# Layer norm 1 of an attention block: the loads of x on another queue, and the order of all engines by hand up to the first values

## The chip, the core and the metric

The kernel runs on one core of a Trainium2 chip. A core has five engines with instruction streams of their own: TensorE (PE in the profile, its weight loads apart as PEld), VectorE (DVE), ScalarE (ACT), GpSimd (POOL) and SyncE (SP), which here only issues DMAs. ACT and GpSimd can issue DMAs as well. The metric is the device time of one execution in microseconds (us), the median of several runs; less is better.

## What is computed

The reference is a network of two layers on x of shape (4, 16, 16, 1024) in float32, seen as 1024 tokens of 1024 channels. What matters for the change is the seam between them:

```python
x = x + conv_attention(group_norm(x), ...)      # layer 0: its last step is a sum of two products per token tile
t = to_tokens(x)                                # 1024 tokens x 1024 channels
t = t + attention(layer_norm(t), W_attn, b_attn, W_proj, b_proj)   # layer 1
t = t + experts(layer_norm(t), ...)             # 8 experts, gates under a threshold are dropped
```

In `attention`, q, k and v are products of the normalised tokens with the three parts of `W_attn`; v is computed first. The result is `y @ W_proj.T + b_proj`, added to t.

## The kernel before, in words

The tokens are handled in eight tiles of 128; tile `t = 2 * b + nt` is half `nt` of image `b`. Layer 0 ends with position terms that are moved by many small DMAs within the chip's memory (`move`, L472, on SP's queue, from `two_T` to `s0`), with a v product of seven half-size products (L513 to L556, the Strassen-Winograd scheme, which reads `xn` and `w_kv`), and then with the loop L575.

Ahead of that loop, x itself is loaded again, one tile per DMA (L564, SP's queue), into memory that `xn` held; so a load can start only when the last v product has read `xn`. The loop goes over the tiles in the order of `tiles` (all tiles with nt = 1, then those with nt = 0). For the tile at place i it does:

- `content` (L437) for the next tile: four products whose results DVE adds to `s0` (L445). For i = 0 it does the first tile's too.
- the spread products `py` (L586): eight matrix products in two banks of PSUM, which DVE adds to x (L593).
- `layer_norm` (L184): statistics on DVE, a square root on ACT between two small DVE steps (`inverse_root`, L131), and the normalising on ACT. The rows have to be turned, so that channels lie on partitions. For the first six tiles the rows are written to DRAM (L207), read back as four quarters (`quarters_of`, L174; both on SP's queue), and turned on DVE in blocks of 32 (`turn`, L179) two tiles later. For the last two, PE transposes them (L202) and ACT copies them out (L203).
- GpSimd adds the bias `b_proj` of the output projection to x (L603) and writes the result to DRAM (`x_rows`, L604), from where it comes back late in layer 1 (L877).

In this loop SP and DVE keep the order in which the code stands (`manual_schedule`); PE, ACT and GpSimd are ordered by a planner. After it, `project_v` (L650) computes v for two halves of the weights, r = 0 and 1. Each is again done with seven products per pair of token tiles: products 1 and 2 need only weights and tokens, 3 to 7 need sums. The sums of weights (`sums_of_A`, L151) are four DVE operations of 128x1024 for each r and are issued after the last layer norm. The sums of tokens (`sums_of_B`, L630) are four DVE operations of 128x2048, and write `T`, which lies where x lay. Each bank goes through `product` (L638), which takes turns between the tags `mm` and `tr`, three banks each. The weights `w_v` are loaded by SP (L121 through L648); the second of them takes the memory of `ln_rows`.

The steps 28 to 33 of layer 1's loop (L867) load x back and run the output projection (`project_out`, L821), which adds its product to x (L827).

```python
            for t in in_time:
                c11, c12, c21, c22 = homes(t)
                nc.scalar.copy(c22, one(t, 1, a11, b11))
                nc.vector.tensor_add(c11, one(t, 2, a12, b21), c22)
            if r == 0:
                sums_of_B()
```

Of the kernel before, what the change touches and what calls it, by code (L numbers as in the profile page):

```python
# [32 lines left out]
F32 = mybir.dt.float32  # L33
I32 = mybir.dt.int32
AF = mybir.ActivationFunctionType
ALU = mybir.AluOpType
# [3 lines left out]
P = 128  # L40
C = 1024
NC = C // P
B = 4
M = 256
# [18 lines left out]
Q = 4  # L63
# [6 lines left out]
def kernel(  # L70
# [54 lines left out]
    def mm(name):  # L125
        return ps.tile([P, HALF], F32, tag="mm", name=name)

    def tr(name):
        return ps.tile([P, HALF], F32, tag="tr", name=name)
# [21 lines left out]
    def sums_of_A(a11, a12, a21, a22, s1, s2, s4):  # L151
        nc.vector.tensor_add(s1, a21, a22)
        nc.vector.tensor_sub(s2, s1, a11)
        nc.vector.tensor_sub(s4, a12, s2)
        nc.vector.tensor_sub(a21, a21, a11)
# [28 lines left out]
    def layer_norm(ln, t, dst, quarters, turns):  # L184


        stats = small.tile([P, 2, 6], F32, tag="ln_stats", name=f"ln1_stats{t}")
        for j in range(2):
            nc.vector.bn_stats(stats[:, j, :], xs[t][:, ts(j, HALF)])
        mv = small.tile([P, 2], F32, tag="ln_mv", name=f"ln1_mv{t}")  # L190
        nc.vector.bn_aggr(mv, stats)
        rstd = small.tile([P, 1], F32, tag="ln_rstd", name=f"ln1_rstd{t}")
        inverse_root(rstd, mv[:, 1:2], EPS)
        if quarters is None:
            less = small.tile([P, 1], F32, tag="ln_less", name=f"ln1_less{t}")
            done = nc.vector.scalar_tensor_tensor(less, mv[:, 0:1], -1.0, rstd, ALU.mult, ALU.mult)
            for j in range(2):
                nc.scalar.activation(ln[:, ts(j, HALF)], xs[t][:, ts(j, HALF)], AF.Identity, bias=less, scale=rstd)
            for j in range(2):
                pt = tr(f"ln1_pt{t}_{j}")  # L200
                for c in range(4):
                    nc.tensor.transpose(pt[:, ts(c, P)], ln[:, (4 * j + c) * P : (4 * j + c + 1) * P], ident)  # L202
                nc.scalar.copy(dst[:, 4 * j : 4 * j + 4, ts(t, P)], pt.rearrange("p (c n) -> p c n", c=4))  # L203
            return done
        done = normalised(ln, xs[t], mv[:, 0:1], rstd)
        rows = turns.tile([P, Q, C // Q], F32, tag="rows", name=f"ln1_rows{t}")
        nc.sync.dma_start(rows.rearrange("n f c -> n (f c)"), ln)  # L207
        quarters_of(rows, quarters)
        return done


    with ExitStack() as layer0:
# [347 lines left out]
        xs = [x_at[:, t, :] for t in range(NT)]  # L560
        tiles = [(b, nt) for nt in (1, 0) for b in range(B)]
        for b, nt in tiles:
            t = 2 * b + nt
            nc.sync.dma_start(xs[t], x[ts(t, P), :])  # L564
# [9 lines left out]
        with tc.manual_schedule(engines={mybir.EngineType.SP, mybir.EngineType.DVE}):  # L574
            for i, (b, nt) in enumerate(tiles):  # L575
                if i == 0:
                    content(b, nt)
                if i + 1 < NT:
                    content(*tiles[i + 1])
                t = 2 * b + nt  # L580
                for hp in range(2):
                    py = mm(f"py{t}_{hp}")
                    for hl in range(2):
                        bh = b * HEADS0 + 2 * hp + hl
                        for mh in range(2):
                            nc.tensor.matmul(  # L586
                                py[:, ts(hl, M)],
                                s0[:, mh, ts(nt, S2), :, bh].rearrange("p i j -> p (i j)"),
                                v_T[:, mh, ts(b, M)],
                                start=(mh == 0),  # L590
                                stop=(mh == 1),
                            )
                    nc.vector.tensor_add(xs[t][:, ts(hp, HALF)], xs[t][:, ts(hp, HALF)], py)  # L593

                quarters = None
                if i < NT - 2:
                    quarters = tpool.tile([P, Q, C // Q], F32, tag="xg", name=f"ln1_quarters{t}")
                to_turn.append((t, quarters))
                ln_done = layer_norm(ln_rows[:, i % 3, :], t, ln1, quarters, turns)
                if i >= 2:  # L600
                    of, quarters = to_turn[i - 2]
                    turn(ln1[:, :, ts(of, P)], quarters)
                nc.gpsimd.tensor_add(xs[t], xs[t], bp)  # L603
                nc.gpsimd.dma_start(x_rows[ts(t, P), :], xs[t])  # L604
    x_home.close()


    with ExitStack() as attention:
        l1, l1w = pool(attention, "l1"), pool(attention, "l1w", 2)
        turns = attention.enter_context(tc.tile_pool(name="turns", bufs=3, space=bass.MemoryType.DRAM))  # L610
        mask = l1.tile([P, 3, P], F32, tag="mask", name="mask")
        nc.gpsimd.memset(mask[:, 1, :], 0.0)
        make_causal_mask(nc, mask[:, 0, :], NEG)
        make_causal_mask(nc, mask[:, 2, :], NEG)
        bqk = l1.tile([P, 2 * NPAIR], F32, tag="bqk", name="bqk")
        nc.gpsimd.dma_start(bqk, b_qk)
        step_qk = l1.tile([P, NPAIR], F32, tag="step_qk", name="step_qk")
        nc.gpsimd.tensor_sub(step_qk, bqk[:, NPAIR:], bqk[:, :NPAIR])

        bv = l1.tile([P, NPAIR], F32, tag="bv", name="bv")  # L620
        nc.gpsimd.dma_start(bv, b_v.rearrange("(n p) -> p n", p=P))
        v1 = [l1.tile([P, NT, M], F32, tag=f"v1_{g}", name=f"v1_{g}") for g in range(4)]


        sums = ExitStack()
        s_pool = pool(sums, "s_pool", 2, side="right")
        T = [s_pool.tile([P, NC // 2, HALF], F32, tag=f"T{i}", name=f"T{i}", bufs=1) for i in range(3)]
        b11, b12, b21, b22 = (ln1[:, 4 * j : 4 * j + 4, ts(l, HALF)] for j in range(2) for l in range(2))

        def sums_of_B():  # L630
            nc.vector.tensor_sub(T[0], b12, b11)
            nc.vector.tensor_sub(T[1], b22, T[0])
            nc.vector.tensor_sub(b12, b12, b22)
            nc.vector.tensor_sub(T[2], b21, T[1])
# [3 lines left out]
        def product(name, stationary, moving, n):  # L638
            nonlocal n_products
            n_products += 1  # L640
            bank = (mm if n_products % 2 else tr)(name)[:, :n]
            for c in range(NC // 2):
                nc.tensor.matmul(bank, stationary(c), moving(c), start=(c == 0), stop=(c == NC // 2 - 1))  # L643
            return bank


        s_v = big_tile(0, "s_v", (2, 3, NC // 2, M))
        w_v = [w_tile(f"w_v{r}", W_attnT[:, 2 * C + r * HALF : 2 * C + (r + 1) * HALF]) for r in range(2)]  # L648

        def project_v(r):  # L650
            a = [w_v[r][:, 4 * j : 4 * j + 4, ts(i, M)] for i in range(2) for j in range(2)]
            a11, a12, s3, a22 = a
            s1, s2, s4 = (s_v[:, r, i, :, :] for i in range(3))
            with tc.issue_after(ln_done.ins):
                sums_of_A(*a, s1, s2, s4)

            def one(t, n, a, b):
                return product(f"pv{r}_{t}_{n}", lambda c: b[:, c, ts(t, P)], lambda c: a[:, c, :], M)

            def homes(t):  # L660
                return [v1[2 * r + i][:, 4 * l + t, :] for i in range(2) for l in range(2)]

            in_time = (1, 3, 0, 2)
            for t in in_time:
                c11, c12, c21, c22 = homes(t)
                nc.scalar.copy(c22, one(t, 1, a11, b11))  # L666
                nc.vector.tensor_add(c11, one(t, 2, a12, b21), c22)
            if r == 0:
                sums_of_B()

            for t in in_time:
                nc.scalar.copy(homes(t)[1], one(t, 3, s4, b22))
            for t in range(4):
                c11, c12, c21, c22 = homes(t)
                nc.vector.tensor_add(c22, one(t, 6, s2, T[1]), c22)
                nc.vector.tensor_add(c21, one(t, 7, s3, b12), c22)
                nc.vector.tensor_add(c12, c12, c22)
                p5 = one(t, 5, s1, T[0])
                nc.vector.tensor_add(c12, p5, c12)
                nc.vector.tensor_add(c22, p5, c21)  # L680
                nc.vector.tensor_add(c21, one(t, 4, a22, T[2]), c21)
# [134 lines left out]
        project_v(0)  # L816
        project_v(1)
# [48 lines left out]
        with tc.manual_schedule():  # L866
            for i in range(written, len(steps) + lag):  # L867
                if i == written:
                    w_p.append(w_tile("w_p0", W_projT[:, :HALF]))
                if i == 28:  # L870
                    w_p.append(w_tile("w_p1", W_projT[:, HALF:]))
                    sums.close()
                    x_pool = pool(x_home, "xb", side="right")
                    xs = [x_pool.tile([P, C], F32, tag=f"x{t}", name=f"xb{t}") for t in range(NT)]
                if 28 <= i < 32:
                    for t in range(2 * (i - 28), 2 * (i - 28) + 2):
                        nc.gpsimd.dma_start(xs[t], x_rows[ts(t, P), :])  # L877
                s_T = turned_s.pop(i - lag)
# [19 lines left out]
                if i == 22:  # L898
                    sums_qk(7)

# [693 lines left out]
```

## Time and profile before

| | before |
|---|---|
| median of 3 runs | 1251.93 us (1250.96 to 1254.14) |
| the profiled execution | 1253.85 us |
| its span in the profile | 1252.0 us |
| PE busy | 1225.3 us (98%) |
| DVE busy | 744.2 us (59%) |
| ACT busy | 220.2 us (18%) |
| GpSimd (POOL) busy | 383.3 us (31%) |
| mean granted TensorE clock | 0.993 |
| stretch of the loop over tiles | about 206 to 277 us |
| first product on weight sums | 297.82 us |

How to read the lines of the profile. A timeline row has the start, the duration, the engine (SPq and ACTq are DMA issues on SP's and ACT's queues), the line of the kernel, the operation, what is written <- what is read, and the count of merged instructions; in brackets stands the idle time just before it and what ended it. PE rows count one float32 product of the code as two records. A row of the windows table has the stretch, its length, the busy time and count of PE, PEld, DVE, ACT and POOL, the granted TensorE clock (1.00 is full), the mean share in which the 16 DMA engines were busy, and GB/s.

### The profile page before, as it was taken

The page shows a single profiled execution, that of the slowest core. Times are in us where ns is not written, and L with a number is a line of the kernel's source. Part 1 is how long each engine was busy: PE and PEld are TensorE (multiplying, and loading weights), DVE is VectorE, ACT ScalarE, POOL GpSimd, SP SyncE. Part 2 cuts the span into 40 slices and gives each one's busy share as a digit, 9 for nine tenths or more (in the row PEclk, how much of TensorE's full clock was granted, in tenths as well). Part 3 has the DMA queues.
Part 4 walks back from the last instruction along what each step waited for, and adds up shares of the span by engine and source line. Part 5 has one row for each costly group of instructions (what it writes and reads, how often), then busy time and mean ns, then how long its engine had stood idle before and what let it go on. Part 6 is the DMA issues. An engine that isn't in the chain of part 4 may idle for free.

```text
span 1252.0 us, 13310 instructions
## 1 busy us (share of the span) xinstructions
PE 1225.3 (98%) x4796; PEld 633.7 (51%) x4796; DVE 744.2 (59%) x1337; ACT 220.2 (18%) x514; POOL 383.3 (31%) x455
## 2 busy tenths in 40 slices
PE   9999999699999999999999999999999999999998
PEld 5445885477885444444444444444344434434443
DVE  5796535487332566666644866864746646565642
ACT  3310111121000222232212422110110111111110
POOL 0141340241000222223231104445543635363520
PEclk9999999889999999999999999999999999999999
DMA  9002023862202344453283558374756485546442
GB/s 348 20 1 84 1 56 74 308 202 101 68 1 68 98 134 133 136 169 113 96 262 119 190 201 285 73 224 94 235 126 190 101 236 151 150 124 197 101 84 53
DMA packets 93977, 169.25 MB, mean 135 GB/s; under 512 B 11952, under 2 KB 48832, under 8 KB 93904
## 3 DMA queue, kind: packets, MB, share of 16 engines
q1 hardware_dynamic: 76544, 115.83, 28.1%
q0 software_dynamic: 15136, 47.78, 16.1%
q10 hardware_dynamic: 2224, 4.72, 1.1%
q8 instruction: 40, 0.66, 0.2%
q14 instruction: 33, 0.27, 0.1%
HBM read 115.59 MB, written 48.50 MB: 131 GB/s over the span
## 4 chain that ended last, share of the span: by engine, by line
PE 74%; DVE 2%; ACT 1%; issue 0%; DVEq 0%; ACTq 0%
PE p L1361 31%; PE pqk L643 16%; PE pv L643 7%; PE po L825 7%; PE left L1403 3%; PE sc L738 2%; PE pa L807 2%; PE rest L1417 2%; PE last_pe L1519 1%; PE dense_pe L945 1%; PE parts L1083 0%; ACT L134 0%; DVE row_T L179 0%; DVE xb L827 0%; DVE T L1304 0%
## 5 line engine op out<-in xcount | busy, mean ns | idle before, releaser
L930 POOL DMA_INDIRECT w_e_xg<-rows,gather x146 | 157.0, 1076 | 57.5 <-issue 39.9
L1361 PE MATMUL p<-w_e,A 128*128 128x512 f32 x368 | 163.2, 593 | 1.3 <-DVE slot L1196 1.3
L780 POOL TENSOR_TENSOR s_q<-s_q,total 128x128 f32<-128x128 f32 (+1 forms) x128 | 66.0, 546 | 301.0 <-DVE total L777 301.0
L825 PE MATMUL po<-w_p,y_T 128*128 128x512 f32 x256 | 118.5, 605 | 0.0
L1361 PEld LDWEIGHTS p<-w_e,A 128*128 128x128 f32 x368 | 69.6, 190 | 89.9 <-issue 89.4
L1361 PE MATMUL p<-T,S 128*128 128x512 f32 x256 | 112.7, 593 | 0.0
L953 POOL DMA_INDIRECT out_dram<-y,add x32 | 56.5, 1766 | 177.4 <-ACT y L1367 114.1
L1367 ACT ACTIVATE y<-y,slot 128x512 f32<-128x512 f32 x64 | 46.1, 722 | 334.6 <-DVE y L1375 175.9
L766 ACT ACTIVATE s_q<-s,top 128x256 f32<-128x256 f32 (+1 forms) x128 | 56.6, 443 | 186.1 <-issue 146.7
L643 PE MATMUL pqk<-ln,w_qk 128*128 128x512 f32 x192 | 85.6, 595 | 0.0
L1361 PEld LDWEIGHTS p<-T,S 128*128 128x128 f32 x256 | 48.6, 190 | 60.8 <-issue 60.5
L825 PEld LDWEIGHTS po<-w_p,y_T 128*128 128x128 f32 x256 | 45.9, 190 | 47.9 <-issue 46.9
L179 DVE STREAM_TRANSPOSE A<-w_e_xg 128x1024 f32<-128x1024 f32 x32 | 39.6, 1239 | 47.8 <-DMA w_e_xg<-rows,gather 47.8
L643 PE MATMUL pqk<-T,S_qk 128*128 128x512 f32 x128 | 58.5, 599 | 0.0
L643 PEld LDWEIGHTS pqk<-ln,w_qk 128*128 128x128 f32 x192 | 36.0, 190 | 43.3 <-issue 42.3
L1361 PE MATMUL p<-w_e,S 128*128 128x512 f32 x128 | 57.5, 592 | 0.0
L1361 PE MATMUL p<-T,A 128*128 128x512 f32 x128 | 57.5, 592 | 0.0
L643 PE MATMUL pv<-w_v,ln 128*128 128x256 f32 x192 | 45.6, 391 | 0.5 <-ACT v L666 0.5
L304 PE MATMUL pq<-w_q,xn 128*128 128x512 f32 x96 | 44.5, 599 | 0.3 <-ACT xn L284 0.3
L603 POOL TENSOR_TENSOR x_at<-x_at,ln_rows 128x1024 f32<-128x1024 f32 x8 | 19.4, 2427 | 78.5 <-ACT ln_rows L162 73.4
L1403 PE MATMUL left<-w_e,one 128*32 128x512 f32 x312 | 41.8, 593 | 0.0
L643 PEld LDWEIGHTS pv<-w_v,ln 128*128 128x128 f32 x192 | 37.3, 196 | 6.4 <-ACT v L666 1.2
(318 smaller groups left out, 1869.2 us busy)
## 6 DMA issues: line engine op xcount, KB each, us to landing
w_e<-in_expert_w_dram SPq DMA_DIRECT2D x14, 2048.0 KB, 12.5
s_rows<-s_q SPq DMA_DIRECT2D x32, 384.0 KB, 2.4
s_rows<-s_rows SPq DMA_DIRECT2D x128, 96.0 KB, 2.3
w_qk<-in_W_attnT_dram SPq DMA_DIRECT2D x8, 1024.0 KB, 5.9
xn<-in_xT_dram SPq DMA_DIRECT2D x8, 512.0 KB, 7.6
w_q<-in_Wq_dram SPq DMA_DIRECT2D x16, 256.0 KB, 7.3
x_at<-in_x_dram SPq DMA_DIRECT2D x8, 512.0 KB, 6.5
w_v<-in_W_attnT_dram SPq DMA_DIRECT2D x2, 2048.0 KB, 13.4
```

The costliest lines, as they stand in the source:

```text
L179: nc.vector.transpose(row_T[:, :, :slots].rearrange("p c (g j) -> p g c j", j=32), row[:, : slots // 32, :].rearrange("p g (c i) -> p g c ...
L304: nc.tensor.matmul(pq, xn[:, c, ts(t, P)], w_q[kc][:, c, :], start=(c == 0), stop=(c == NC - 1))
L643: nc.tensor.matmul(bank, stationary(c), moving(c), start=(c == 0), stop=(c == NC // 2 - 1))
L738: nc.tensor.matmul(psc[:, h, qt * P : qt * P + (qt + 1) * P], qk[pair][part, 0, b * M + qt * P : b * M + (qt + 1) * P], qk[pair][part, 1, ...
L766: nc.scalar.activation(blocks(h, qt), s[:, h, cols].rearrange("p (b f i) -> p b f i", f=Q, i=32), AF.Exp, bias=top[:, qt, h : h + 1], accu ...
L780: nc.gpsimd.tensor_mul(blocks(h, qt), blocks(h, qt), total[:, qt, h : h + 1].unsqueeze(2).unsqueeze(3).to_broadcast([P, 1 + qt, Q, 32]),)
L825: nc.tensor.matmul(po, y_T[:, c, ts(t, P)], w_p[j][:, c, :], start=(c == 0), stop=(c == NC - 1))
L930: nc.gpsimd.indirect_dma_start(out=row[:, g, :], out_offset=None, in_=table[: (TOK - P) * Q, :] if e in SHORT else table, in_offset=bass.I ...
L953: nc.gpsimd.indirect_dma_start(out=out[: TOK - P, :] if e in SHORT else out, out_offset=bass.IndirectOffsetOnAxis(ap=add[:slots, e, k : k ...
L1361: nc.tensor.matmul(bank, a[:, c, :], b[:, c, :], start=(c == 0), stop=(c == NC // 2 - 1))
L1367: nc.scalar.mul(y[i][:, ts(j, HALF)], y[i][:, ts(j, HALF)], slot[:, e, 1, 2 * pair + i : 2 * pair + i + 1])
L1403: nc.tensor.matmul(bank[ts(i, 32), :], stationary, w[of][j][:, c, :], start=(c == 0), stop=(c == NC - 1))
```

## The change

- The eight loads of x are issued by ACT and no longer by SP.
- The order by hand covers all engines, and reaches from the loop over tiles to the end of r = 0 of the values and the start of GpSimd's work for r = 1 (`in_order`).
- `layer_norm` is cut into parts: the norm itself, `turn_by_rows`, `turn_on_pe` and `turned_on_pe`. The loop runs over seven tiles; the eighth is done by steps in between the first products of the values: products 1 and 2 for tiles 1 and 3, then the transposes of the seventh tile, products for tile 0, the transposes of the eighth, products for tile 2.
- The sums of weights are done by GpSimd (`sums_v`), those for r = 0 right after the last spread products, the others later. The mask and the small bias loads of GpSimd stand after the first of them.
- The sums of tokens are done in two halves (`sums_of_B(1)`, `sums_of_B(0)`), eight operations in place of four.
- The quarters of the first four tiles use memory of layer 0 that is free (`spare`), the next two a pool of their own (`late`).
- For the last two tiles in the order, x is written to `x_rows` by SP right after the spread products, without the bias. GpSimd adds the bias after x has come back, at steps 32 and 33; the bias is loaded once more at step 28.
- The first `w_v` load stands ahead of the loop in the code; `w_v1` comes after the transposes.

The diff, cut to its core:

```diff
-    def sums_of_A(a11, a12, a21, a22, s1, s2, s4):
-        nc.vector.tensor_add(s1, a21, a22)
...
+    def sums_of_A(a11, a12, a21, a22, s1, s2, s4, engine=nc.vector):
+        engine.tensor_add(s1, a21, a22)
...
+    def turn_by_rows(ln, t, quarters, turns):
         rows = turns.tile([P, Q, C // Q], F32, tag="rows", name=f"ln1_rows{t}")
         nc.sync.dma_start(rows.rearrange("n f c -> n (f c)"), ln)
         quarters_of(rows, quarters)
...
+    def turn_on_pe(ln, banks):
+
+        for j, pt in enumerate(banks):
+            for c in range(4):
+                nc.tensor.transpose(pt[:, ts(c, P)], ln[:, (4 * j + c) * P : (4 * j + c + 1) * P], ident)
+
+    def turned_on_pe(dst, t, banks):
+        for j, pt in enumerate(banks):
+            nc.scalar.copy(dst[:, 4 * j : 4 * j + 4, ts(t, P)], pt.rearrange("p (c n) -> p c n", c=4))
...
+        late = pool(x_home, "late", 2, side="right")
...
-            nc.sync.dma_start(xs[t], x[ts(t, P), :])
+            nc.scalar.dma_start(xs[t], x[ts(t, P), :])
...
-        with tc.manual_schedule(engines={mybir.EngineType.SP, mybir.EngineType.DVE}):
...
+        w_v = [w_tile("w_v0", W_attnT[:, 2 * C : 2 * C + HALF])]
+        in_order.enter_context(tc.manual_schedule())
+        for i in range(NT - 1):
+            t = spread(i)
+            quarters = None
+            if i < NT - 2:
+                if i < NT - 4:
+                    quarters = spare[i % 2]
+                else:
+                    quarters = late.tile([P, Q, C // Q], F32, tag="xg", name=f"ln1_quarters{t}")
+            to_turn.append((t, quarters))
+            layer_norm(ln_rows[:, i % 3, :], t, i >= NT - 2)
+            if i >= 2:
+                turn_quarters(i - 2)
+            if i < NT - 2:
+                turn_by_rows(ln_rows[:, i % 3, :], t, quarters, turns)
                 nc.gpsimd.tensor_add(xs[t], xs[t], bp)
                 nc.gpsimd.dma_start(x_rows[ts(t, P), :], xs[t])
+            else:
+                nc.sync.dma_start(x_rows[ts(t, P), :], xs[t])
+        t = spread(NT - 1)
+        nc.sync.dma_start(x_rows[ts(t, P), :], xs[t])
+        s_v = big_tile(0, "s_v", (2, 3, NC // 2, M))
...
+        def first(r, t, *tags):
+            nc.scalar.copy(homes(r, t)[3], one(r, t, 1, *tags[:1]))
+            return r, t, one(r, t, 2, *tags[1:])
+
+        def second(r, t, bank):
+            c11, c12, c21, c22 = homes(r, t)
+            nc.vector.tensor_add(c11, bank, c22)
...
+        sums_v(0, nc.gpsimd)
+        seconds = [first(0, 1, tr, tr), first(0, 3, mm, tr)]
+        layer_norm(ln_rows[:, (NT - 1) % 3, :], t, True)
+        two = ps.tile([P, 2, HALF], F32, tag="sc", name="ln_two", bufs=1)
+        banks = two[:, 0, :], two[:, 1, :]
+        turn_on_pe(ln_rows[:, (NT - 2) % 3, :], banks)
+        turned_on_pe(ln1, to_turn[NT - 2][0], banks)
+        turn_quarters(NT - 3)
+        for done in seconds:
+            second(*done)
+        second(*first(0, 0, mm, mm))
+        banks = tr("ln_pt0"), mm("ln_pt1")
+        turn_on_pe(ln_rows[:, (NT - 1) % 3, :], banks)
+        turned_on_pe(ln1, t, banks)
+        second(*first(0, 2, tr, tr))
+        x_home.close()
...
+        w_v.append(w_tile("w_v1", W_attnT[:, 2 * C + HALF :]))
+
+        in_time = (1, 3, 0, 2)
+        odd, even = sums_of_B(1), sums_of_B(0)
+        next(odd), next(odd), next(even)
+        for t in in_time:
+            nc.scalar.copy(homes(0, t)[1], one(0, t, 3))
+        for t in in_time:
+            others_v(0, t)
+            if t == 1:
+                next(even)
...
+        sums_v(1, nc.gpsimd)
...
+        in_order.close()
...
+                    bp = pool(bp_home, "bp", side="right").tile([P, C], F32, tag="bp", name="bp")
+                    nc.gpsimd.dma_start(bp, b_proj.partition_broadcast(P))
...
+                if 32 <= i < 34:
+                    b, nt = tiles[NT - 34 + i]
+                    t = 2 * b + nt
+                    nc.gpsimd.tensor_add(xs[t], xs[t], bp)
```

## Prediction, made before the change was run

> **What bounds the kernel now.** I read the page's first part (PE busy 1225.3 of a span of 1252.0 us, so at most 26.7 us of standing time in all), then the windows table over the stretch that the change touches, then the timelines of PE, of SP's queue and of DVE there. Windows first (columns: PE, PEld, DVE, ACT, POOL busy and instructions, granted clock, DMA share, GB/s):
>
> ```profile
> 210.00:220.00 10.00, 9.93 (x31) 6.09 (x29) 1.62 (x3) 0.00 (x0) 0.00 (x0) 1.00 0.36 82
> 220.00:230.00 10.00, 3.41 (x9) 2.79 (x10) 3.78 (x10) 0.78 (x2) 0.00 (x0) 0.66 0.73 264
> 240.00:260.00 20.00, 16.15 (x48) 10.96 (x47) 10.36 (x22) 2.89 (x4) 5.80 (x4) 0.83 0.68 241
> 280.00:300.00 20.00, 17.64 (x75) 14.49 (x76) 11.55 (x14) 4.65 (x10) 5.56 (x5) 0.91 0.46 159
> ```
>
> Three holes in PE, each with a lowered clock. PE's timeline shows them:
>
> ```profile
> 216.34 3.60 PE L437 MATMUL pc<-q,k_q 128*128 128x512 f32 x8
> 226.59 5.31 PE L586 MATMUL py<-v_T,s 128*128 128x256 f32 x16 [6.66 <-DVE x_at L593]
> 231.74 3.60 PE L437 MATMUL pc<-q,k_q 128*128 128x512 f32 x8
> 235.17 3.71 PE L586 MATMUL py<-v_T,s 128*128 128x256 f32 x16
> 251.40 3.78 PE L437 MATMUL pc<-q,k_q 128*128 128x512 f32 x4 [3.85 <-DVE s L445]
> 286.30 1.36 PE L202 MATMUL ln_pt<-ident,ln_rows 128*128 128x128 f32 x8 [1.85 <-ACT ln_rows L198]
> 287.50 10.49 PE L643 MATMUL pv<-w_v,ln 128*128 128x256 f32 x40
> 297.82 7.07 PE L643 MATMUL pv<-s_v,ln 128*128 128x256 f32 x32
> ```
>
> Each hole ends at DVE or ACT, but those waited too. SP's queue, from its timeline, shows what the loads stand behind (start, duration of the issuing, count):
>
> ```profile
> 199.73 22.23 SPq L472 DMA_DIRECT2D s<-two_T  x35
> 222.08 3.95 SPq L564 DMA_DIRECT2D x_at<-in_x_dram  x8
> 226.07 0.47 SPq L121 DMA_DIRECT2D w_v<-in_W_attnT_dram  x1
> 230.69 0.33 SPq L207 DMA_DIRECT2D ln_rows<-ln_rows  x1
> 244.45 1.85 SPq L174 DMA_DIRECT2D ln_quarters<-ln_rows  x4
> ```
>
> And DVE's timeline names in brackets what it waited for and how long:
>
> ```profile
> 225.85 1.28 DVE L593 TENSOR_TENSOR x_at<-x_at,py 128x512 f32<-128x512 f32 x2 [12.17 <-DMA x_at<-in_x_dram]
> 249.53 1.25 DVE L179 STREAM_TRANSPOSE ln<-ln_quarters 128x1024 f32<-128x1024 f32 x1 [7.67 <-DMA ln_quarters<-ln_rows]
> 284.99 0.16 DVE L135 RECIPROCAL ln_rstd<-ln_rstd 128x1 f32<-128x1 f32 x1 [3.68 <-ACT ln_rstd L134]
> ```
>
> First hole: the x loads stand behind 35 moves in SP's queue, 22.23 us of issuing while the DMA engines are a third busy. Second: 4.2 MB of x and 2.1 MB of weights then fill the DMA engines, and tile 0's normalised rows, written to DRAM at 230.69, can be read back only from 244.45. Third: tile 7's square root waits on ACT behind copies that wait for PE.
>
> **What is there to win.** A content group takes 3.43 (231.74 to 235.17) and a spread group 3.54 (235.17 to 238.71). Eight of each are 55.8; PE took 71.2, from 205.92 to 277.15: 15.5 lost (6.66 and 3.85 standing, the rest mostly groups at half clock: 5.31 and 4.71 for 3.71, 3.78 for 1.88). Up to the first product on weight sums PE then does 8 products at 1.73 (four take 6.9 from 297.82) and 16 transposes, 0.44 for four: 15.6, against 20.7 taken: 5.1 lost. In sum **20.5 us**. Work behind it is dense on PE, so what is won here reaches the end.
>
> **Part by part.**
>
> *x on ACT's queue.* xn's memory is free at the end of the last v product, 205.9. Eight issues at 0.44 are 3.5 us of ACT. At worst the last of the v_T activations (0.81) stands behind them and ends at 210.3; PE wants it at 212.8, so it is hidden. The first tile landed 3.8 after its issue: about 211 now, wanted by the first x add at 214.8. The loads (10.5 us at 400 GB/s) share the engines with the moves and end about 220, far ahead of one tile per 7 us. The first hole goes. A rule speaks against this: the Trainium skill, "DMA: Bandwidth & Descriptors", section "Issuing engines are not separate DMA queues", says that a second issuing engine saves only the sequencer's time, usually small beside the transfer. By it I would book little. The row has 22.23 us of sequencer time ahead of the first x tile, so I book the whole hole; the same rule tells me that w_v and the rows get no more bandwidth.
>
> *The rows of tile 0.* What is late next. SP still issues moves until 222.1, then w_v (0.47), so rows 0 leaves at 222.6 although ACT has it ready at about 220.8. Ahead of or beside it lie w_v, itself and the first x_rows write: 3.1 MB, 7.9 us at 400 GB/s, and 1 for completion: 231.5. The four quarters took 5.1 from issue to DVE: 236.6. DVE wants to turn tile 0 at 233.4 (py2 starts at 226.7 in a dense PE, and before the turn was wanted 6.7 after it). With PE's order by hand, content 5 needs the bank that DVE frees 1.9 after the turn begins (turn 1.25, one add 0.65); PE arrives at 237.2. So PE stands 236.6 + 1.9 - 237.2 = 1.3. Ends: without x_rows in the way, rows lands at 229.2 and nothing is lost; with the 13.8 us of before, PE stands 6.1. I take 1.3, since x is out of the way. From tile 1 on, rows took 4.6 to their quarters' issue and less later, with 1.8 of issuing: 6.4 on SP, under the 7.0 of a tile.
>
> *The clock after it.* The Trainium skill, "TensorE: Matmul & The Clock Gate", "What's actually happening", has the clock halve only after an idle window of some 3.4 us: 1.3 would then cost nothing more. In this trace standing times of 0.46 and 1.85 were followed by a clock of 0.50 at 288 to 290, and the 40 products took 10.3 where 8.6 is dense. I go by the row: 1.7. Residue 3.0.
>
> *The tail by hand, all engines.* PE does tiles 1 and 3 first (6.9), then tile 6's transposes, tile 0, tile 7's transposes, tile 2. Tile 7: statistics done 264.4; its root now stands behind two copies, the later at 266.9, as in the row with 3.68, but PE has other work: normalised at 269.9, wanted at 273.0. Tile 6 and the turns of tiles 0 and 2 have more room. Booked: the whole 5.1. If that cover were gone, 2 to 5 come back. The new holding of "sc" and "tr" banks costs nothing for the same reason.
>
> *Weight sums on GpSimd.* They leave DVE (7.0 in all). GpSimd takes 2.36 to 2.91 for 128x1024 with two operands (its bias adds), so the third, s4, comes 7.1 to 8.7 after the last spread product frees its memory (261.7): at most 270.4, wanted at 277.3. The second set needs w_v1, issued at about 273, landed by 287, done by 298, wanted after 312. Beside a GpSimd add one DVE sum took 3.37 for 1.22; DVE's work in that stretch has PSUM or one operand, and such rows beside GpSimd kept their 1.27. Mask and bias loads moved behind the sums have over 100 us. Zero; 2 to 4 if DVE's B sums collide and the banks run out.
>
> *B sums in halves:* eight at about 1.22 for four at 2.29; the first two are done near 280, PE needs them at 284. Their memory waits for x_rows; those two writes go out right after the adds: done about 267. Zero.
>
> *Bias of two tiles later:* one 512 KB load and two adds of 2.36 between 662 and 680, where GpSimd idles for 18.0; the tiles are wanted after 690. Zero; 1 to 3 if it weren't so. More quarter buffers: zero or a small gain.
>
> Sum: 20.5 - 3.0 = 17.5. The profiled execution took 1253.85 (span 1252.0 and 1.85 around it); it becomes 1236.35. It lies 1.92 above the median of 1251.93, so the median becomes **1234.4**.
>
> **Rivals.**
> *No residue* (25%): rows 0 lands by 230 and the whole 20.5 is won: 1231.4. For it: x leaves earlier. Against: w_v is ahead in the same queue.
> *The read-back takes the place of the x wait* (18%): the moves are issued more slowly beside x, or the round trip keeps its 13.8. PE stands 6.1, and 2.9 go to the clock (as after 3.85): gain 11.5, 1240.4.
> *The tail's loss stays* (7%): copies, roots or sums by hand block each other, 5.1 lost: 1239.5.
> *x no sooner* (3%): ACT issues it only after something late; first hole stays: about 1244.
> *Slower* (5%, of it 2% near no change): SP's in-order round trip bounds all tiles. Writing a tile's rows must take so long that a tile's period is 10.4 instead of 7.0 (rows landing in 8.2 rather than 4.6, six tiles): from there the 20.5 is eaten. At 11.4: about 1258. Against it: the later landings of before, 2.7 to 4.6.
> The forecast has 42% (1232.5 to 1236.5).
>
> Range 1230.5 to 1241.5: from the full gain, with some 0.9 of spread, to just past the read-back case; the last two rivals and part of the tail's and read-back's spread stay outside. About 0.3% is what a measurement here tells from no change. Faster by more: all cases but the last, 0.95; within it 0.02 and slower 0.03, both from the last.
>
> **What would show it.** Right: 8 loads of x on ACT's queue near 206; no DVE wait for x; PE dense from 206 to about 237; rows 0 issued near 222.6, its quarters near 231.5; DVE waiting about 3 for them; first product on weight sums near 280; GpSimd's s4 done before it. Wrong: moves still issued at 225 or later, a DVE wait over 6 for quarters, PE waiting for ACT or GpSimd in the tail.

## The result, and the profile after

| | before | after |
|---|---|---|
| median | 1252.99 us (1250.96 to 1254.14, 4 runs) | 1245.93 us (1245.57 to 1246.28, 4 runs) |
| the profiled execution, its span | 1253.85, 1252.0 us | 1245.87, 1244.1 us |
| loop over tiles on PE | 205.92 to 277.15: 71.2 us | 206.43 to 273.68: 67.25 us |
| from there to the first product on weight sums | 20.7 us | 16.07 us |

The ratio is 0.9945, with a 95% interval of 0.9928 to 0.9963: faster by 7 us where 17.5 were forecast, and outside the range of 1230.5 to 1241.5. (The forecast started from a median of 1251.93 for before; a fourth run, 1254.05, moved it to 1252.99.) The windows of after, in the same four stretches and columns as before:

```profile
210.00:220.00 10.00, 3.89 (x11) 1.78 (x9) 2.06 (x3) 0.24 (x1) 0.00 (x0) 0.95 0.36 83
220.00:230.00 10.00, 9.38 (x24) 6.42 (x25) 3.77 (x10) 2.54 (x4) 0.00 (x0) 0.71 0.95 326
240.00:260.00 20.00, 18.32 (x61) 12.53 (x60) 14.15 (x30) 3.63 (x6) 6.57 (x6) 1.00 0.74 237
280.00:300.00 20.00, 19.76 (x100) 17.31 (x99) 12.91 (x11) 5.69 (x12) 11.77 (x11) 1.00 0.32 107
```

The tail (280 to 300) is dense now. The first hole is as large as it was and only lies 6 us earlier: from 210 to 220 PE works 3.89 of 10. The timeline, rows of PE, ACT, SP's queue and DVE one after the other, shows where it comes from:

```profile
213.30 0.59 PE L595 MATMUL py<-v_T,s 128*128 128x256 f32 x2
220.62 5.88 PE L595 MATMUL py<-v_T,s 128*128 128x256 f32 x14 [6.73 <-ACT v_T L557]
...
249.11 3.70 PE L444 MATMUL pc<-q,k_q 128*128 128x512 f32 x8 [1.68 <-DVE s L452]
...
289.75 7.07 PE L656 MATMUL pv<-s_v,ln 128*128 128x256 f32 x32
...
205.12 0.81 ACT L557 ACTIVATE v_T<-v_T,vp 128x512 f32<-128x512 f32 x1 [0.38 <-DVE v_T L552]
219.32 0.39 ACTq L572 DMA_DIRECT2D x_at<-in_x_dram  x1
219.76 0.81 ACT L557 ACTIVATE v_T<-v_T,vp 128x512 f32<-128x512 f32 x1 [13.83 <-DMA s<-two_T]
220.51 6.85 ACTq L572 DMA_DIRECT2D x_at<-in_x_dram  x7
...
222.38 0.53 SPq L121 DMA_DIRECT2D w_v<-in_W_attnT_dram  x1
237.06 0.35 SPq L204 DMA_DIRECT2D ln_rows<-ln_rows  x1
242.56 1.83 SPq L174 DMA_DIRECT2D emb<-ln_rows  x4
...
247.24 1.25 DVE L179 STREAM_TRANSPOSE ln<-emb 128x1024 f32<-128x1024 f32 x1 [3.78 <-DMA emb<-ln_rows]
```

x is on ACT's queue, yet its first load leaves at 219.32, not near 206: before it was 222.08. And PE does not wait for x. It waits for the last of the v_T activations, which stands behind that load on ACT and was held for 13.83 us. The bracket names what held it: a DMA from `two_T` to `s`, one of the small moves on SP's queue, with which neither x nor v_T has anything to do. Further down, tile 0's rows leave SP at 237.06, 14.7 us after w_v, though ACT had them ready at 230.8. The list of SP's waits (us in all, times, longest) names the reason:

```profile
SPq L204 <- DMA w_v<-in_W_attnT_dram: 14.1, 1, 14.1
```

Both are explained by the semaphores that the built program waits for (no time is in this list; first ACT's, then SP's):

```
L572 DMACopy x_at<-in_x_dram 128x1024 [waits DMAHW6_49,PE_49]
L557 Activation v_T<-v_T,vp 128x512 [waits DVE_49]
L572 DMACopy x_at<-in_x_dram 128x1024 [waits DMAHW0_49]
L572 DMACopy x_at<-in_x_dram 128x1024 [waits DMAHW1_49]
...
L479 DMACopy s_892<-two_T 16x256 [waits DMAHW5_49]
L121 DMACopy w_v_1490<-in_W_attnT_dram 128x8x512 [waits DMAHW7_49,PE_49]
L204 DMACopy ln_rows_1534<-ln_rows 128x1024 [waits DMAHW7_49,Activation_49]
```

In this program, as it was built, the DMAs issued by SP and ACT report their landing on eight counters, DMAHW0 to 7, handed out in turn in the order of the program; a DMA waits until the one before it on its counter has landed. The first x load takes the counter (DMAHW6) of the eighth move from the end. That one was issued at 217.3 (221.69 less seven moves of 0.63) and landed 2.0 later: 219.3, the very time at which x leaves. Rows 0 got the counter of w_v, eight DMAs earlier. DMAs of GpSimd have counters of their own (DMASW).

### The profile page after: what moved, and what is told of

Read it like the earlier page. It is cut to its first block, busy times and chain, and to the rows that moved or that the text cites. A ratio compares the mean times of both kernels' runs of the same rounds, so it can differ in the third digit from the quotient of the medians.

```text
span 1244.1 us, 13324 instructions
## 1 busy us (share of the span) xinstructions
PE 1222.2 (98%) x4796; PEld 633.7 (51%) x4796; DVE 741.6 (60%) x1333; ACT 220.0 (18%) x514; POOL 404.0 (32%) x462
## 4 chain that ended last, share of the span: by engine, by line
PE 89%; SPq 4%; DVE 3%; DMA 2%; ACT 1%; issue 1%; POOL 0%; DVEq 0%; ACTq 0%; POOLq 0%
PE p L1440 31%; PE pqk L656 16%; PE pv L656 8%; PE po L897 7%; SPq L479 4%; PE pq_pair L392 4%; PE left L1482 3%; PE pq L311 3%; PE pk L423 2%; PE sc L812 2%; PE pa L881 2%; PE rest L1496 2%; PE pT L502 1%; DMA w_v<-in_W_attnT_dram 1%; PE py L595 1%; PE last_pe L1598 1%
## 5 line engine op out<-in xcount | busy, mean ns | idle before, releaser
L1440 PEld LDWEIGHTS p<-w_e,S 128*128 128x128 f32 x128 | 24.3, 190 | 30.6 <-issue 30.6
L1440 PEld LDWEIGHTS p<-T,A 128*128 128x128 f32 x128 | 24.3, 190 | 30.6 <-issue 30.1
```

Of the source, the lines that this page charges most:

```text
L1440: nc.tensor.matmul(bank, a[:, c, :], b[:, c, :], start=(c == 0), stop=(c == NC // 2 - 1))
```

## The experiments

The theory: the eight shared counters tie ACT's loads to SP's moves. Rivals: ACT itself is late; the bytes of x and w_v (6.3 MB) bind whatever queue they are in; SP's time to issue the moves binds. All kernels were timed against the kernel before. Edits are against the changed kernel unless said. The last column is the time from the first product of the loop over tiles to the first product of the values; with the planner's order the two are mixed, so it has none.

| kernel | median us | ratio to before (95%) | loop on PE, us |
|---|---|---|---|
| after | 1245.93 | 0.9945 (0.9928 to 0.9963) | 67.25 |
| x on GpSimd | 1245.81 | 0.9942 (0.9925 to 0.9959) | 67.0 |
| x on SP | 1250.87 | 0.9987 (0.9979 to 0.9994) | 71.7 |
| last v_T on DVE | 1248.38 | 0.9961 (0.9947 to 0.9975) | 70.0 |
| w_v on GpSimd | 1247.15 | 0.9954 (0.9937 to 0.9970) | 67.7 |
| x and w_v on GpSimd | 1240.44 | 0.9898 (0.9882 to 0.9915) | 61.5 |
| x on GpSimd, w_v late on SP | 1243.31 | 0.9923 (0.9906 to 0.9939) | 64.1 |
| x, w_v and rows 0 on GpSimd | 1242.92 | 0.9924 (0.9907 to 0.9940) | 65.0 |
| x, and w_v late, on GpSimd | 1242.03 | 0.9910 (0.9890 to 0.9930) | 64.0 |
| as that, half of x late | 1248.08 | 0.9950 (0.9931 to 0.9969) | 68.3 |
| x, w_v and 12 moves on GpSimd | 1234.51 | 0.9860 (0.9843 to 0.9876) | 55.8 |
| order by hand on SP and DVE alone | 1250.39 | 0.9982 (0.9972 to 0.9992) | |
| weight sums of r = 0 on DVE | 1246.07 | 0.9945 (0.9929 to 0.9962) | 67.8 |

### x on GpSimd's queue

```diff
-            nc.scalar.dma_start(xs[t], x[ts(t, P), :])
+            nc.gpsimd.dma_start(xs[t], x[ts(t, P), :])
```

> The changed kernel with the eight loads of x on GpSimd's queue. Theory (the DMAs of SP's and ACT's queues take eight completion counters in turn, and one is issued only when the eighth before it has landed; so x on ACT is tied to the last moves on SP): GpSimd's DMAs have counters of their own, x starts near 206 to 207, DVE does not wait for x, ACT's last v_T activation is no longer late, PE is dense from 206 to about 237, rows 0 leaves SP near 223 without waiting for w_v, and the median falls by 8 to 10 us, to 1236 to 1238. Rival (x is late because the memory of xn or the DMA engines are busy till about 219): x starts no sooner and the time stays within 1 us of 1245.9.

Its timeline (POOL, SP's queue, DVE, PE):

```profile
206.85 4.21 POOL L572 DMA_DIRECT2D x_at<-in_x_dram  x8 [23.31 <-PE pv L530]
...
199.50 27.08 SPq L479 DMA_DIRECT2D s<-two_T  x36
...
244.78 1.25 DVE L179 STREAM_TRANSPOSE ln<-emb 128x1024 f32<-128x1024 f32 x1 [11.12 <-DMA ln_rows<-ln_rows]
...
246.65 5.62 PE L444 MATMUL pc<-q,k_q 128*128 128x512 f32 x8 [9.02 <-DVE s L452]
```

Off the shared counters, x leaves at 206.85, when its memory is free, and the first hole is gone: the counters, not the memory, had held x. The time did not move. x's 4.2 MB now land while SP issues moves; 36 of them take 27.08 us where 35 took 22.23 before, since a move issued beside x lands after 6.2 (median from 205 on) instead of 2.0, and the next on its counter waits for that. So w_v leaves at 226.68 and rows 0 at 227.31, 4.7 later than I had booked; its quarters are issued only at 237.88, and one hole of 9.02 takes the place of 6.73 and 1.68. This is my rival "the read-back takes the place of the x wait". Of the two ways that it named, the first came in full (the moves are issued more slowly beside x) and the second in part: the round trip from rows 0 to its quarters' issue took 10.6, where 8.9 were booked and the rival had 13.8.

### x back on SP's queue

```diff
-            nc.scalar.dma_start(xs[t], x[ts(t, P), :])
+            nc.sync.dma_start(xs[t], x[ts(t, P), :])
```

> The changed kernel with the loads of x back on SP. Theory: x starts at about 222 in place of 219.3, the v_T activation is no longer late, but PE still stands some 6 to 7 for x, and x and w_v then fill the DMA engines to 241, so tile 0's quarters come at about 249 and PE, ordered by hand, stands 4 to 6 there: the first stretch is as long as before, the gain of the tail (4.6) stays, 1248 to 1250.5. Rival (the queue of x is what gained, the tail nothing): 1252 to 1253. Rival (the queue of x gained nothing at all): 1245.9.

```profile
227.58 5.91 PE L595 MATMUL py<-v_T,s 128*128 128x256 f32 x16 [6.93 <-DVE x_at L602]
...
252.13 5.40 PE L444 MATMUL pc<-q,k_q 128*128 128x512 f32 x8 [4.72 <-DVE s L452]
```

The two holes of before are back (6.93 and 4.72 for 6.66 and 3.85), the tail is as short as after the change (16.07), and the rest of the change alone is worth 1.7 us in the median, 3.1 in the span. ACT's queue gave 5 of the 7 us.

### The last v_T activation on DVE

```diff
+                if (j, th) == (1, 0):
+                    nc.vector.tensor_scalar(v_T[:, j, ts(th, HALF)], v_T[:, j, ts(th, HALF)], vp[:, 0, j : j + 1], vp[:, 1, j : j + 1], ALU.mult, ALU.add)
+                    continue
```

> The changed kernel with the last of the four v_T activations done by DVE, so that it does not stand behind the waiting x load on ACT. Theory (two waits in line: the v_T one hides the one behind it, since rows 0 is held on SP until w_v has landed): the first hole shrinks from 6.7 to about 4 and moves to the second tile's spread products, but the read-back of tile 0 still comes at about 247, the hole there grows by what the first loses: within 1 us of 1245.9. Rival (the late v_T activation is the whole loss): 2.5 to 4 us are won, 1242 to 1243.5.

```profile
223.78 5.23 PE L605 MATMUL py<-v_T,s 128*128 128x256 f32 x16 [3.85 <-DVE x_at L612]
230.45 3.70 PE L444 MATMUL pc<-q,k_q 128*128 128x512 f32 x8 [1.44 <-DVE s L452]
...
248.63 6.39 PE L444 MATMUL pc<-q,k_q 128*128 128x512 f32 x8 [3.98 <-DVE s L452]
```

v_T no longer stands behind x, PE goes on to the end of the first tile's products, and waits there for x itself (3.85). ACT has nothing left to do then, and x still leaves only at 218.97: it was not ACT's own work that held it. Rows 0 still stand behind w_v's counter until 236.8, and as PE gets to the fifth content product 2.8 sooner than in after, the read-back is now 3.98 late. Two holes with a slow clock after each instead of one: slower than after by 2.4, where I had expected no more than 1 either way. The wait of v_T was only the first of three, one behind the other.

### w_v on GpSimd's queue

```diff
-        w_v = [w_tile("w_v0", W_attnT[:, 2 * C : 2 * C + HALF])]
+        w_v = [w_tile("w_v0", W_attnT[:, 2 * C : 2 * C + HALF], queue=nc.gpsimd)]
```

> The changed kernel with the first load of w_v on GpSimd's queue. Theory: rows 0 then waits for no load; it leaves SP when it is normalised, near 231 in place of 237, tile 0's quarters are there before DVE wants them at 243.5, the second hole (1.7) goes, the first (6.7) stays: 1243.5 to 1244.5. Rival (rows 0 is held by full DMA engines and not by the counter): DVE still waits 2 to 4 for the quarters, 1245.5 to 1246.

```profile
199.53 25.85 SPq L479 DMA_DIRECT2D s<-two_T  x37
...
223.74 4.78 PE L595 MATMUL py<-v_T,s 128*128 128x256 f32 x14 [10.20 <-ACT v_T L557]
```

Rows 0 no longer wait for w_v: they leave at 234.13, and the hole at the fifth content product is gone. But w_v's 2.1 MB now lie beside the moves, which are issued later, and x on ACT waits for their counters: it leaves at 222.43 and the first hole grows from 6.73 to 10.20. Both couplings are shown, and again one wait uncovers the other: 1247.15, where 1243.5 to 1244.5 was expected.

### x and w_v on GpSimd's queue

Both edits above together.

> The changed kernel with x and then the first w_v both on GpSimd's queue. Theory (two things stand ahead of tile 0's rows, one at a time: x behind the moves, and w_v ahead of the rows on SP; with only one removed, the other takes the whole gain): with both gone rows 0 leaves SP right after the moves, near 228, its quarters are turned by 236, PE stands under 1.5 there and nowhere else in the loop, and the median is 1235 to 1238. Rival (the bytes bound it: x, w_v, moves and rows need the DMA engines until about 240 in any order): quarters not before 242, a hole of 7 or more, 1243 to 1246.

Timeline (SP's queue, DVE, PE):

```profile
200.04 28.77 SPq L479 DMA_DIRECT2D s<-two_T  x37
229.54 0.37 SPq L204 DMA_DIRECT2D ln_rows<-ln_rows  x1
235.81 1.87 SPq L174 DMA_DIRECT2D emb<-ln_rows  x4
...
240.36 1.25 DVE L179 STREAM_TRANSPOSE ln<-emb 128x1024 f32<-128x1024 f32 x1 [5.83 <-DMA emb<-ln_rows]
...
242.23 5.40 PE L444 MATMUL pc<-q,k_q 128*128 128x512 f32 x8 [3.73 <-DVE s L452]
```

Faster than after by 5.5, yet short of what I expected: the moves now take until 228.8, so rows 0, ready at 221.8, leave at 229.54. One hole of 3.73 is left, and 1.8 for the clock after it. Is it the bytes or SP's issuing that is late? The next five runs ask that.

### w_v late on SP's queue, x on GpSimd's

```diff
-        w_v = [w_tile("w_v0", W_attnT[:, 2 * C : 2 * C + HALF])]
+        w_v = []
...
+                if i == 2:
+                    w_v.append(w_tile("w_v0", W_attnT[:, 2 * C : 2 * C + HALF]))
```

> x on GpSimd's queue, and the first w_v on SP's queue after the third tile's quarters. Theory: rows 0 leaves SP after the moves, near 227, its quarters are turned by 235; w_v then delays the fourth tile's rows by some 5, for which there is room: PE stands under 2 in the loop, 1235 to 1238. Rival (the bytes bound it): the hole only moves to the fourth tile, 4 or more there, 1240 to 1245.

```profile
238.95 3.70 PE L444 MATMUL pc<-q,k_q 128*128 128x512 f32 x8 [1.29 <-DVE s L452]
...
264.99 5.44 PE L595 MATMUL py<-v_T,s 128*128 128x256 f32 x16 [4.85 <-DVE s L452]
```

With w_v out of the way the first read-back is 1.29 late. But rows 3 now stand behind w_v on SP (issued 246.85, their quarters at 258.58), and 4.85 is lost there. Putting a load off only chose another tile to pay.

### x, w_v and rows 0 on GpSimd's queue

Tile 0's rows and quarters too are issued by GpSimd (`turn_by_rows` and `quarters_of` with `queue=nc.gpsimd` for i = 0).

> x, the first w_v, and the rows and quarters of the first tile alone on GpSimd's queue. Theory (what is left in the version with x and w_v on GpSimd's queue is that SP still issues moves until 229 when tile 0's rows are ready at 221): rows 0 leaves at 221 to 222, its quarters are turned when DVE wants them (near 234), no hole above 1 in the loop, and the 5.7 of the hole and its clock are won: 1234 to 1236. Rival (the DMA engines are full until 240, whoever issues): the quarters are turned at 239 or later, PE stands 3 or more: 1239 to 1241.

```profile
234.43 2.23 POOL L174 DMA_DIRECT2D emb<-ln_rows  x4 [12.34 <-issue]
...
243.97 6.59 PE L444 MATMUL pc<-q,k_q 128*128 128x512 f32 x8 [6.07 <-DVE s L452]
```

Rows 0 leave 8 us earlier, at 221.55, and gain nothing by it: it is 12.9 us to the quarters' issue, and they are turned at 242.10, 1.7 later than with x and w_v alone there. I first took this for the bytes' doing, since the DMA engines were busy throughout (share 1.03 and 1.04 from 210 to 228). The run with twelve moves on GpSimd speaks against that.

### x, and w_v late, on GpSimd's queue; and half of x late

As two kernels above, but the late w_v is issued by GpSimd; then also only four x tiles at once, and one more after the rows of each of the first four tiles:

```diff
+        for i in range(4):
+            load_x(i)
...
+                if i < 4:
+                    load_x(i + 4)
```

> x on GpSimd's queue, the first w_v on GpSimd's queue too but only after the third tile's normalised rows have been written. Theory (what decides is the bytes ahead of tile 0's read-back, and what stands behind w_v in its own queue): the moves end at about 228, tile 0's quarters are turned at about 237 as with w_v late on SP (a hole of about 1.3), and the second hole of that kernel (4.85 at the fourth tile, with the clock after it) goes, because the fourth tile's rows no longer stand behind w_v on SP: 1236 to 1238. Rival (bytes bind whichever queue they are in): w_v's bytes only move the hole to a later tile, one of 4 or more is seen there: 1240 to 1244.

> As the kernel with w_v late on GpSimd, but only the first four tiles of x are loaded at once, the other four one by one, each after the rows of one of the first four tiles. Theory (the bytes beside the moves lengthen them): the moves end at about 224, tile 0's rows are read back by about 234, no hole above 0.5: 1234.5 to 1236.5. Rival (the moves are as slow beside four tiles as beside eight, or the late tiles of x come late): 1237 or more.

The first, then the second:

```profile
244.40 0.47 SPq L204 DMA_DIRECT2D ln_rows<-ln_rows  x1
256.31 1.73 SPq L174 DMA_DIRECT2D s_w<-ln_rows  x4
...
256.57 6.06 PE L444 MATMUL pc<-q,k_q 128*128 128x512 f32 x8 [5.54 <-DVE s L452]
```

```profile
194.92 31.72 SPq L479 DMA_DIRECT2D s<-two_T  x45
...
241.87 5.40 PE L444 MATMUL pc<-q,k_q 128*128 128x512 f32 x8 [3.65 <-DVE s L452]
...
254.89 6.27 PE L444 MATMUL pc<-q,k_q 128*128 128x512 f32 x8 [4.08 <-DVE s L452]
```

My theory missed twice. With w_v late on GpSimd, PE is dense to 251 (better than the 1.29 expected), then one hole of 5.54: w_v's bytes meet the read-back of a later tile, as the rival said. The fourth tile's rows, on SP's queue, came back for their quarters' issue only after 11.9 (244.40 to 256.31), and the third tile's quarters, issued at 242.38, were turned at 254.70, while w_v was on its way in GpSimd's queue from 237.7 for 14.9 us. With half of x late, the moves end at 226.6, no sooner than beside all of x (226.0), although the DMA engines are only half busy from 216 to 228 (share 0.46 and 0.57). At 0.63 each, 45 moves in 31.7 lost 3.4; beside all of x, 43 in 31.05 lost 4.0. Most of the stall comes with the first tiles, so fewer bytes did not get SP free sooner. Why the quarters of tile 0 then took from 231.98 to 240.00 to be turned, and those of the second tile from 240.95 to 253.02, with the engines at a share of 0.95 to 1.05 from 234 to 258, is not settled.

### Twelve of the moves on GpSimd too

On top of x and w_v on GpSimd's queue:

```diff
-        move(lambda k, ni: True)
+        later = moves[1::2]
+        for m in moves[::2]:
+            nc.sync.dma_start(*m[2:])
...
+        for m in later:
+            nc.gpsimd.dma_start(*m[2:])
```

> As the kernel with x and w_v both on GpSimd's queue, but sixteen or so of the last moves into s are issued by GpSimd, which stands idle until x's memory is free, instead of by SP. At about 0.6 each SP is done with its moves some 9 us earlier. Theory (SP's issue of moves is what holds tile 0's rows once x and w_v have left SP's way): SP ends its moves at about 216 to 219, tile 0's rows leave at 221 where they are ready, instead of 229.5, the quarters are turned by 236, and the 3.73 at the fifth content product with the slow clock after it goes: 1234.5 to 1236.5. Rival (x's and w_v's 6.3 MB, on their way from 208 to 234, hold the read-back whatever SP does): tile 0's quarters are turned at 239 or later, 1239 to 1242. Against both: GpSimd's window copies now stand between moves, so that the stretch before 206 may grow by up to 3.

GpSimd took twelve moves, not sixteen, between its window copies, all before 188. Windows, then the timeline (SP's queue, DVE, PE):

```profile
210.00:216.00 6.00, 6.00 (x19) 3.67 (x18) 2.13 (x4) 0.50 (x1) 3.05 (x6) 1.00 1.02 366
216.00:222.00 6.00, 6.00 (x22) 4.16 (x21) 4.26 (x10) 1.16 (x2) 0.00 (x0) 1.00 1.05 334
222.00:228.00 6.00, 6.00 (x22) 4.30 (x22) 3.47 (x10) 0.48 (x2) 2.92 (x2) 1.00 1.02 390
228.00:234.00 6.00, 6.00 (x24) 4.64 (x23) 3.82 (x7) 1.24 (x1) 2.92 (x2) 1.00 1.05 337
```

```profile
207.14 9.34 SPq L518 DMA_DIRECT2D s<-two_T  x13
222.31 0.37 SPq L204 DMA_DIRECT2D ln_rows<-ln_rows  x1
229.28 1.81 SPq L174 DMA_DIRECT2D emb<-ln_rows  x4
...
235.39 1.25 DVE L179 STREAM_TRANSPOSE ln<-emb 128x1024 f32<-128x1024 f32 x1 [0.44 <-DMA emb<-ln_rows]
...
238.76 3.60 PE L444 MATMUL pc<-q,k_q 128*128 128x512 f32 x8
...
263.24 7.07 PE L660 MATMUL pv<-w_v,ln 128*128 128x256 f32 x32
```

The theory holds, within its numbers: SP is done at 216.5 instead of 228.8 (7.6 us for the twelve moves at 0.63, the rest because fewer are issued beside x), rows 0 leave at 222.31 when ACT has them, are turned at 235.39, and PE has no hole from the loop's start at 207.46 to its end: 55.8 us, the dense time. At 1234.51 it beats both kernels. The DMA engines are as full as in the kernel with x and w_v alone on GpSimd (1.02 to 1.05 from 210 to 234, there 1.00 to 1.04), so it was not the bytes that held tile 0's read-back there. The rows' way from issue to the quarters' issue is 7.0 here and 6.3 there; with rows 0 in one queue with x and w_v, and as long after x's first load (14.4 us in both), it was 12.9. Whether the common queue did that or GpSimd as the issuer is not told apart. The last hole had been SP's time to issue the moves.

### The order by hand on SP and DVE alone

```diff
-        in_order.enter_context(tc.manual_schedule())
+        in_order.enter_context(tc.manual_schedule(engines={mybir.EngineType.SP, mybir.EngineType.DVE}))
```

> The changed kernel with only SP and DVE ordered by hand, as before the change; PE, ACT and GpSimd by the planner. Theory (the tail is won by the order by hand of PE and ACT): the first stretch is as long as after the change or shorter by up to 2, since PE may take half a content group earlier, and the tail loses 3 to 5: 1248 to 1251. Rival (the tail is won by the weight sums leaving DVE): 1245 to 1246.5.

The timeline (PE, DVE):

```profile
293.26 3.62 PE L656 MATMUL pv<-s_v,ln 128*128 128x256 f32 x16
298.60 1.99 PE L656 MATMUL pv<-s_v,T 128*128 128x256 f32 x8 [1.72 <-DVE T L687]
301.89 1.99 PE L656 MATMUL pv<-w_v,ln 128*128 128x256 f32 x8 [1.30 <-DVE ln L689]
...
294.03 1.23 DVE L686 TENSOR_TENSOR T<-ln 128x1024 f32<-128x1024 f32 x1
295.29 3.25 DVE L687 TENSOR_TENSOR T<-ln,T 128x1024 f32<-128x1024 f32 x1
```

4.5 slower than after, and in the range that I had expected, but not for the reason that I gave. The planner mixes products of the values into the loop, so the tail has to be counted by its work: from the loop's first product until the loop, the transposes and products 1 to 3 of r = 0 are all done, PE took 99.0 before (205.92 to 304.89), 90.4 after (206.43 to 296.82) and 91.0 here (205.84 to 296.88). So up to that point the planner's order keeps 7.9 of 8.6 us, and 0.5 of the rest is the first hole, 7.24 for 6.73. It loses 3.6 behind that point, where PE waits twice for DVE's sums of tokens: they start 3.2 later than after (294.03 for 290.86), and three of the first four then take 3.25 to 3.37 beside GpSimd's second set of weight sums, where after the change one of them did. So the order by hand of PE, ACT and GpSimd is worth some 4 us, at the sums of tokens; it is not what shortened the tail.

### Weight sums on DVE

```diff
-        sums_v(0, nc.gpsimd)
+        sums_v(0, nc.vector)
```

> The changed kernel with the first set of weight sums on DVE, at the same place in the order. Theory (the sums on GpSimd matter only by their place: on DVE they stand for 5 to 7 ahead of tile 7's statistics, whose rows PE wants 3 after they are ready): tile 7's transposes come late, PE stands 2 to 4: 1248 to 1250. Rival (there is room on DVE in the tail): 1245.5 to 1246.5.

1246.07 for 1245.93: no difference, where 1248 to 1250 was expected. DVE takes 1.21 to 1.22 for each and has the room, and the tail does not grow by it (15.6); moving the sums to GpSimd is worth nothing by itself. So neither this nor the planner's order takes the tail's gain away. What is left is the layer norm in parts, with the order on DVE and SP that goes with it; that was not tried by itself.

## Why the prediction was wrong, point by point

- **x on ACT's queue: the step that failed.** "xn's memory is free at the end of the last v product, 205.9 ... The first tile landed 3.8 after its issue: about 211 now." I took the memory as the only thing that x waits for. It waited for the counter of a move on SP too, until 219.3. The wrong start cost 6.73 of standing and 2.6 of slow clock (5.88 for 14 records, where 16 dense ones take 3.71): 9.3, in a loop that came out 8.5 worse than forecast (the residue of the read-back was 1.2 smaller than booked). That x leaves at 206.85 on GpSimd's queue shows that the memory was free, as I had said. I had written this case down as "x no sooner", at 3% and 1244, with the right shape ("ACT issues it only after something late") and much too small a chance. Nothing in the timeline of before could have shown the coupling, since x stood on SP itself; the program's own list of waits would have.
- **"At worst the last of the v_T activations stands behind them and ends at 210.3."** The order was right, the bound was not: it was held for 13.83 and ended at 220.6. An activation behind a DMA on its engine inherits all that the DMA waits for.
- **"Rows 0 leaves at 222.6 ... 1.3."** PE stood 1.68, close to it, but by accident: rows 0 left at 237.06, held by w_v's counter, while PE too came 10.2 later than booked (247.43 for 237.2). With x early (on GpSimd) the same step is off by 7.7: 9.02. Of that, 4.7 is that the moves are issued more slowly beside x, which I had as a reason for a rival only; 1.7 is the way to DRAM (10.6 for 8.9; the 400 GB/s in it are what before shows from 226 to 236, 398 to 421, the 1 us for completion is shown by no row) and 1.8 the way back to DVE (6.9 for 5.1), less 0.4 by which PE came later. So the forecast would have failed by this step alone had x left at 206: 1245.81.
- **"The clock after it: 1.7, I go by the row."** Wrong. After 1.68 the clock stayed at 1.00 (3.70 for 8 records, dense 3.60). In these runs single holes of 1.29 to 2.15 cost nothing more, and those from 3.65 upward were followed by whole groups of 5.2 to 6.6 that take 3.6 to 3.7 when dense; none lay between. That is on the side of the rule in the Trainium skill, "TensorE: Matmul & The Clock Gate", "What's actually happening", against which I chose. Two such holes close together, 1.72 and 1.30 with the planner's order, left the clock at 1.00 as well; what differed in the row of before (0.46 and 1.85, with transposes between) was not tried.
- **The tail: right in size, its cause open.** 4.6 of the 5.1 booked came (20.7 to 16.07). I had put it to the order by hand of all engines; with PE, ACT and GpSimd left to the planner PE was as far at 296.88 as after at 296.82.
- **Weight sums, sums of tokens, late bias: zero, right,** the first shown by its own run, the others only by the absence of a wait in PE's rows. For the sums of tokens the zero hangs on the order by hand: with the planner's, PE lost 3.6 there, the "2 to 4 if DVE's B sums collide".
- **What the forecast of 1234.4 needed.** Three couplings had to go: x off the shared counters, w_v off SP's queue and counters, and a part of the moves off SP. That the median was then 1234.51 is chance: the loop took 55.8, 3.0 less than the 58.8 that the forecast had with its residue, and of that 1.5 went to a later start of the loop (207.46 for 205.92) and 0.5 was missing in the tail.

In sum, on the profiled spans: 4.0 of 12.5 in the loop, 4.6 of 5.1 in the tail, less 0.7 elsewhere (0.5 of it a later start of the loop): 7.9.

## What to carry to other kernels

Before a DMA is put on another engine's queue, read in the built program which semaphores it will wait for: with counters handed out in turn, a load on one queue waits for small moves on another, and what stands behind it on its engine waits too. Many small DMAs on one queue are a resource of their own; count how long they take to issue, also beside a bulk load, and what stands behind them. When three waits lie one behind the other, taking away one of them may show nothing (1245.81 for 1245.93) or cost time (1248.38); follow what the next one becomes before calling the first harmless.

## What the runs showed of the hardware that I had not expected

- A move issued beside a bulk load lands after 6.2 to 6.7 us (medians with x, and with x and w_v, on GpSimd) instead of 2.0, and with eight counters the issuing of 37 then takes 28.8 us where some 23 is the undisturbed pace.
- DMA engines that are busy at a share of 1.02 to 1.05 did not hold up a 512 KB write on another queue in one kernel (7.0 us to the quarters' issue, twelve moves on GpSimd), where behind 6.3 MB in the same queue it took 12.9. But another queue is no shelter by itself: with w_v late on GpSimd's queue such a write on SP's took 11.9, at a share of 0.85 to 1.07 from 240 to 254. What tells the two apart is open.
- Beside GpSimd's second set of weight sums, DVE's sums of tokens took 3.25 to 3.38 for 1.22, and GpSimd's own 2.60 to 3.33 for 2.35. In the changed kernel PE did not wait for either; with the planner's order it stood 1.72 and 1.30 for DVE's.
